# A state-space, attention and feed-forward kernel: recurrence steps spread differently over the stages, its carry copy on another engine, and larger weights for the gap in the feed-forward

## The chip, the cores and the metric

The kernel runs on one core of one Trainium2 chip. The metric is the device time of one execution in microseconds (us); the median of 3 runs before the change is 4947.52 us (4943.62 to 4969.08). The core has five engines [...]: PE (TensorE, matrix products), DVE (VectorE), ACT (ScalarE), POOL (GpSimd) and SP (SyncE, which here issues nearly all transfers). [...]

## The reference, cut to what matters

Input is x, 8 images of 384 channels and 32x32 points, in fp32. Layer 0 normalizes x over channels and runs a selective state-space recurrence (Mamba) over the 1024 points, forwards and backwards, beside a 3x3 depthwise convolution:

```
deltaA  = exp(delta[..., None] * A)                     # 16 states per channel
deltaBu = (delta * u)[..., None] * Bm[:, :, None, :]
h = dA * h + dBu ;  y = einsum('bdn,bn->bd', h, c)      # scan over the points
y = (y + u * D) * silu(z) ;  out = y @ out_proj
x = x + res_scale * ((fwd + bwd) * scale_mod + sigmoid(dwconv(xn)) * xn)
```

Layer 1 takes the points as tokens: t += attention(layernorm(t)) with 6 heads and a causal mask, then t += ffn(layernorm(t)). The feed-forward has weights binarized by sign; after each of its two linear maps the values are scaled by 128 over the largest absolute value of their group and clipped. Groups are 8 // 5 = 1 batch wide, so only batches 0 to 4 pass through it (for 5, 6 and 7 it adds zero). The largest value must be known before the first scaled value can be used: once between the two linear maps, ahead of the gelu, and once after the second.

## The kernel before, in words

Channels lie on the 128 partitions in 3 chunks, points along the free dimension in two halves of 512. Each batch passes four stages:

- *Preparation* (`before_scan`): normalization, input projection (`in`), the short convolution (`u`), gates and the 3x3 convolution (`loc`), the projection to the rows B and C (`xp`), then `delta`, which writes delta and delta times u to DRAM for every chunk, direction and half.
- *Recurrence*: 96 units per batch, 768 in all. A unit is one chunk, one direction, one half and two of the 16 states. POOL multiplies (delta u) by the row of B (`s_first`, L592, out `g`, 128x1024); ACT makes the two exponentials in PSUM (L605, `da`); DVE scans each state (L610, in place in `g`, 128x512); POOL multiplies by the row of C (L616, in place); PE transposes and sums into `y` (`s_sum`, L624). Each direction covers its two halves one after the other (`PARTS`). The units of the first half (24 in a row) begin at zero, and a POOL copy (L615) stores the last column of their two states in `carry`; the units of the second half begin from it. That copy and both products of POOL are pinned: they keep their program order.
- *Attention* (`attention`): output projection (`op`), layernorm, `qp`, `vp`, scores `s`, masked and negated by DVE (L801), exponential by ACT, transposes `pt`, weighting `av`, the factors of the softmax (L831 to L840, small DVE operations), output `ap`.
- *Feed-forward* (`feed_forward`, batches 0 to 4): `hp` (L995), its largest value (`quant_scale`, L961 to L967), gelu by ACT (L1018, four instructions), clip by DVE (L1021), `yp` (L1039), the second scale, and the output.

The recurrence is issued through *slots*. Slot k loads for unit k+4, issues the first product of unit k+2, the exponentials, scans, carry copy and second product of unit k, the sum of unit k-1 and the gate of unit k-2. 98 slots (with 4 that only run ahead) go beside the preparation of the first four batches and the binarizing of the weights, a part that the change leaves as it is. The other 672 are laid over the remaining stages by a plan at the end of the kernel. Every step of a stage is emitted with an estimated duration: 2.5 unless it says otherwise (`emit.of`). The batches go in the order 0, 1, 2, 3, 5, 6, 4, 7. For each the plan appends the steps of attention; for batches 0 to 3 also a *joint* stage, in which the feed-forward steps and the preparation of a later batch (5, 6, 4, 7) are merged by `spread_over`, each list evenly over its own sum of estimates:

```
            fed = spread_over(fed, steps_of(before_scan, later.pop(0), ("pt", "pt", "av")))
            fed = [(f, JOINT * us) for f, us in fed]
```

The estimates of a joint stage are multiplied by JOINT = 0.6. Batch 4 has a feed-forward without a preparation beside it. The attention of batch 7 comes last, with no slots. By the due times (unit 96 i must be done before the attention of the i-th batch) the plan finds the steepest straight line, and along each such line puts slots at even distances in estimated time. A slot thus falls where the sum of the estimates puts it. The tile framework then orders the instructions of each engine, with this order as their priority, except what is pinned or raised by `high_priority`.

Of the kernel before, what the change touches and what calls it, by code (L numbers as in the profile page):

```python
# [38 lines left out]
BC0 = 32  # L39
DW = BC0 + 2 * NS  # L40
PARTS = ((0, 0), (0, 1), (1, 1), (1, 0))
JOINT = 0.6
SET = 8
HURRY = 400
AHEAD = 2
# [9 lines left out]
def kernel(  # L55
# [16 lines left out]
    nc = tc.nc  # L72
    pin = tc.keep_in_program_order
# [25 lines left out]
    def bank(name, tag=None):  # L99
        if tag is None:  # L100
            turn[0] += 1
            tag = ("s", "pt")[turn[0] % 2]
        return ps.tile([P, HB], F32, name=name, tag=tag, bufs=BANKS[tag])
# [7 lines left out]
    def load(dst, src):  # L111
        nc.sync.dma_start(out=dst, in_=src)
# [168 lines left out]
    def layernorm(src, name, emit):  # L281

        dst = src
        st = {}
        for h in range(NH):

            @emit.of(6.0)
            def _(h=h):
                mean = mean_of(lambda c: src()[:, c, half(h)], f"mean_{name}_{h}")
                for c in range(NC):  # L290
                    nc.vector.tensor_tensor(
                        dst()[:, c, half(h)], src()[:, c, half(h)], mean, ALU.subtract
                    )
                st[h] = squares(dst(), h, name)

        for h in range(NH):

            @emit.of(6.0)
            def _(h=h):
                var = mean_of(lambda c: st[h][c], f"var_{name}_{h}")  # L300
                rstd_of(var, 1)
                for c in range(NC):
                    nc.vector.tensor_tensor(  # L303
                        dst()[:, c, half(h)], dst()[:, c, half(h)], var, ALU.mult
                    )
# [289 lines left out]
    def s_scan(u):  # L595
        g = sst["g", u.name]
        key = ("carry", u.b, u.c, u.d)
        begins = u.part % 2 == 0
        if begins and u.n == 0:
            sst[key] = sp.tile([P, NS], F32, name=f"carry_{u.name}", tag="carry", bufs=2 * NC)  # L600
        carry = sst[key]
        for i in range(2):
            n = u.n + i
            da = bank(f"da_{u.name}_{i}", "da")
            nc.scalar.activation(  # L605
                da, sst["dl", u.b, u.c, u.part], AF.Exp, scale=amat[:, u.c, n : n + 1]
            )
            first = 0.0 if begins else carry[:, n : n + 1]
            gi, step = g[:, i, :], -1 if u.d else 1
            nc.vector.tensor_tensor_scan(  # L610
                gi[:, ::step], da[:, ::step], gi[:, ::step], first, ALU.mult, ALU.add
            )
        if begins:
            end = 0 if u.d else HB - 1
            pin(nc.gpsimd.tensor_copy(carry[:, u.n : u.n + 2], g[:, :, end]))  # L615
        pin(nc.gpsimd.tensor_tensor(g, g, sst["bc", 1, u.b, u.part, u.n], ALU.mult))  # L616

    def s_sum(u):
# [351 lines left out]
    def feed_forward(b, t, emit):  # L970
        st = {}

        @emit
        def _():
            st["xn"] = t()
            st["mxh"] = small.tile([P, NF], F32, name=f"mxh_{b}", tag="mxh", bufs=1)
            st["mxy"] = small.tile([P, NC], F32, name=f"mxy_{b}", tag="mxy", bufs=1)

        layernorm(t, f"nf_{b}", emit)
        for m in range(NF):  # L980
            for h in range(NH):

                @emit.of(3.1)
                def _(m=m, h=h):
                    if m % NC == 0 and h == 0:
                        st["h", m // NC] = btile(f"h{m // NC}_{b}")
                    if m % 2 == 0 and h == 0:
                        st["w1"] = mtile(f"w1_{b}_{m}").rearrange("p (c e) -> p c e", c=4)
                        load(
                            st["w1"][:, :NC, :],  # L990
                            w1s[:, m * P : (m + 2) * P].rearrange("(c p) e -> p c e", p=P),
                        )
                    hp = bank(f"hp_{b}_{m}_{h}", "s")
                    for c in range(NC):
                        nc.tensor.matmul(  # L995
                            out=hp,
                            lhsT=st["w1"][:, c, chunk(m % 2)],
                            rhs=st["xn"][:, c, half(h)],
                            start=(c == 0),
                            stop=(c == NC - 1),  # L1000
                        )
                    hm = st["h", m // NC][:, m % NC, :]
                    nc.scalar.activation(hm[:, half(h)], hp, AF.Identity, bias=b1t[:, m : m + 1])
                    if h == NH - 1:
                        nc.vector.tensor_reduce(
                            st["mxh"][:, m : m + 1], hm, AX.X, ALU.max, apply_absolute_value=True
                        )

        @emit.of(3.0)
        def _():  # L1010
            st["s1"] = quant_scale(st["mxh"], f"h_{b}")


        @emit.of(3.0)
        def _():
            with tc.high_priority(offset=60):
                for q in range(NF // NC):
                    pin(nc.scalar.activation(st["h", q], st["h", q], AF.Gelu, scale=st["s1"]))  # L1018
                pin(nc.scalar.preload_act_table_set(LOG_EXP))
                for q in range(NF // NC):  # L1020
                    nc.vector.tensor_scalar(st["h", q], st["h", q], QCLIP, None, ALU.min)  # L1021

        for m in range(NC):
            for h in range(NH):

                @emit.of(10.7)
                def _(m=m, h=h):
                    if m == 0 and h == 0:
                        st["y"] = btile(f"yf_{b}")
                    if h == 0:  # L1030
                        for k in range(0, NF, 6):
                            w = mtile(f"w2_{b}_{m}_{k}", 6 * P).rearrange("p (k e) -> p k e", k=6)
                            load(
                                w, w2s[k * P : (k + 6) * P, chunk(m)].rearrange("(k p) e -> p k e", p=P)
                            )
                            st["w2", k // 6] = w
                    yp = bank(f"yp_{b}_{m}_{h}", "s")
                    for k in range(NF):
                        nc.tensor.matmul(  # L1039
                            out=yp,  # L1040
                            lhsT=st["w2", k // 6][:, k % 6, :],
                            rhs=st["h", k // NC][:, k % NC, half(h)],
                            start=(k == 0),
                            stop=(k == NF - 1),
                        )
                    ym = st["y"][:, m, :]
                    nc.scalar.activation(
                        ym[:, half(h)], yp, AF.Identity, bias=vec[:, m, V_B2 : V_B2 + 1]
                    )
                    if h == NH - 1:  # L1050
                        nc.vector.tensor_reduce(
                            st["mxy"][:, m : m + 1], ym, AX.X, ALU.max, apply_absolute_value=True
                        )

        @emit.of(3.0)
        def _():
            st["s2"] = quant_scale(st["mxy"], f"y_{b}")

        for m in range(NC):

            @emit
            def _(m=m):
                to = mtile(f"t3_{b}_{m}")
                load(to, spilled[b, "t2", m])
                for h in range(NH):
                    ym = bank(f"yq_{b}_{m}_{h}", "s")
                    nc.vector.tensor_scalar(
                        ym, st["y"][:, m, half(h)], st["s2"], QCLIP, ALU.mult, ALU.min
                    )
                    th = to[:, half(h)]  # L1070
                    nc.vector.scalar_tensor_tensor(th, ym, -QCLIP, th, ALU.max, ALU.add)
                nc.sync.dma_start(out=out[b, chunk(m), :], in_=to)


    class Steps(list):
# [4 lines left out]

        def of(self, us):
            return lambda f: self(f, us)

    def spread_over(*lists):

# [64 lines left out]
    for i, b in enumerate(ORDER):  # L1150
        if i > 0:
            due.append((sum(us for _, us in rest), i * per))
        fed = Steps()
        rest += steps_of(attention, b, fed) if i < B - 1 else []
        if fed and later:
            fed = spread_over(fed, steps_of(before_scan, later.pop(0), ("pt", "pt", "av")))
            fed = [(f, JOINT * us) for f, us in fed]
        rest += fed

    timed, here = [], 0  # L1160
# [63 lines left out]
```

## Time and profile before

| | us |
|---|---|
| median of 3 runs | 4947.52 |
| the profiled execution, its own time | 4952.38 |
| its span, first to last instruction | 4950.6 |
| busy PE, DVE, ACT, POOL | 4007.3, 3659.0, 2669.5, 3696.7 |
| start, until the first attention | 829 |
| attention of batches 0, 1, 2, 3, 5, 6 (windows) | 333, 344, 355, 358, 343, 352 |
| joint stages after batches 0, 1, 2, 3 | 324, 327, 315, 328 |
| attention and feed-forward of batch 4 | 322, 210 |
| attention of batch 7, alone | 210 |

An engine's busy time is the time in which one of its instructions runs, its waits for semaphores left out. A group of instructions stands as one line: line of the program, engine, operation, output and inputs by name, shapes, count, then busy time, the mean duration of one, the idle time of the engine just before them and what ended it. The busy shares come in 40 equal slices of the span, as digits in tenths, 9 for 90% and more; a slice is 124 us. The stages in the table were cut at the first output projection of each attention and at the last of its `ap` products.

### The profile page before, as it was taken

How to read it: one execution, taken by the hardware profiler on the slowest of the kernel's cores; microseconds unless marked ns; L12 is line 12 of the kernel's file. 1: busy time of each engine (PE TensorE's matmuls, PEld its weight loads, DVE VectorE, ACT ScalarE, POOL GpSimd, SP SyncE). 2: the span in 40 equal slices, each digit the busy share in tenths (PEclk: the TensorE clock that was granted, in tenths of full speed). 3: DMA queues.
4: the chain of work that ended last, by engine and by line, in shares of the span. 5: the costliest groups of instructions: out<-in, count | busy, mean ns of one | idle time of the engine just before them, and what ended most of it. 6: DMA issues, size and time to landing. Idle time of an engine off the chain costs nothing. (4 is left out here: it accounts for less than half of the span.)

```text
span 4950.6 us, 50616 instructions
## 1 busy us (share of the span) xinstructions
PE 4007.3 (81%) x16362; PEld 2168.0 (44%) x16362; DVE 3659.0 (74%) x4818; ACT 2669.5 (54%) x4855; POOL 3696.7 (75%) x1944
## 2 busy tenths in 40 slices
PE   4677786988788788688887888887887988988889
PEld 1243343544444444344443444443454444444444
DVE  6887878677887778786778967687867677676623
ACT  4565655564654655545655446565456365464425
POOL 0487787996878986768876699867799888888800
PEclk7787796999989899888898998898899989989999
DMA  6554546333454334363343634334643334334210
GB/s 228 204 177 165 196 157 238 107 102 124 150 198 137 115 124 165 126 207 114 108 135 128 220 121 135 111 128 153 203 128 119 114 112 140 117 103 139 92 61 26
DMA packets 365009, 696.35 MB, mean 141 GB/s; under 512 B 30104, under 2 KB 88904, under 8 KB 364744
## 3 DMA queue, kind: packets, MB, share of 16 engines
q1 hardware_dynamic: 355232, 676.97, 41.4%
q10 hardware_dynamic: 9512, 16.15, 0.9%
q8 instruction: 129, 2.11, 0.2%
q14 instruction: 136, 1.11, 0.1%
HBM read 527.33 MB, written 165.68 MB: 140 GB/s over the span
## 5 line engine op out<-in xcount | busy, mean ns | idle before, releaser
L592 POOL TENSOR_TENSOR g<-ud,bc 128x1024 f32<-128x1024 f32 x768 | 1843.2, 2400 | 518.7 <-PE y L624 391.9
L616 POOL TENSOR_TENSOR g<-g,bc 128x1024 f32<-128x1024 f32 x768 | 1821.0, 2371 | 271.1 <-DVE g L610 196.1
L605 ACT ACTIVATE da<-dl,amat 128x512 f32<-128x512 f32 x1536 | 1056.9, 691 | 1457.7 <-DVE g L610 1436.7
L610 DVE TENSOR_TENSOR_SCAN g<-da,g 128x512 f32<-128x512 f32 x768 | 907.5, 1211 | 423.5 <-POOL g L592 411.8
L610 DVE TENSOR_TENSOR_SCAN g<-da,carry,g 128x512 f32<-128x512 f32 x768 | 953.7, 1272 | 348.4 <-POOL g L592 322.9
L624 PE MATMUL y<-ident,g 128*128 128x128 f32 x6144 | 938.7, 301 | 249.2 <-POOL g L616 122.2
L624 PEld LDWEIGHTS y<-ident,g 128*128 128x128 f32 x6144 | 782.0, 155 | 696.7 <-issue 379.8
L787 PE MATMUL s<-k,q 64*128 64x512 f32 (+3 forms) x1152 | 388.4, 600 | 121.6 <-DVE nm L801 103.5
L801 DVE CUSTOM_DVE_ANT_0 pr<-s,cmask 128x512 f32<-128x512 f32 (+3 forms) x576 | 300.3, 546 | 168.4 <-PE s L787 167.1
L811 ACT ACTIVATE pr<-pr,nm 128x512 f32<-128x512 f32 (+3 forms) x576 | 349.9, 609 | 123.6 <-DVE nm L801 121.9
L863 PE MATMUL pt<-ident,pr 128*128 128x128 f32 x1728 | 301.9, 307 | 98.1 <-ACT ptn L866 78.5
L995 PE MATMUL hp<-t,w 128*128 128x512 f32 x720 | 335.7, 611 | 38.7 <-DMA w<-w1s 30.8
L1039 PE MATMUL yp<-h,w 128*128 128x512 f32 x720 | 331.7, 619 | 19.2 <-DMA w<-w2s 15.1
L863 PEld LDWEIGHTS pt<-ident,pr 128*128 128x128 f32 x1728 | 216.2, 154 | 240.2 <-ACT ptn L866 134.5
L877 PE MATMUL av<-ptn,v 128*64 128x512 f32 (+3 forms) x1152 | 270.8, 551 | 49.7 <-ACT ptn L866 35.8
L342 PE MATMUL in<-xn,win 128*128 128x512 f32 x576 | 282.7, 637 | 26.8 <-DVE xc L464 8.2
L866 ACT COPY ptn<-pt 128x512 f32<-128x512 f32 (+3 forms) x576 | 255.6, 474 | 62.0 <-PE pt L863 60.0
L401 DVE SCALAR_TENSOR_TENSOR loc<-xn,vec,loc 128x496 f32<-128x496 f32 (+3 forms) x384 | 259.6, 722 | 20.1 <-ACT loc L390 18.8
L729 PE MATMUL qp<-t,wqk 128*128 128x512 f32 x576 | 263.3, 607 | 10.3 <-DVE t L303 6.5
L615 POOL COPY carry<-g 128x2 f32<-128x2 f32 x384 | 85.7, 223 | 214.8 <-DVE g L610 214.6
L787 PEld LDWEIGHTS s<-k,q 64*128 64x128 f32 x1152 | 132.2, 207 | 257.9 <-DVE nm L801 174.9
L1039 PEld LDWEIGHTS yp<-h,w 128*128 128x128 f32 x720 | 141.8, 201 | 194.0 <-issue 169.8
(151 smaller groups left out, 4714.2 us busy)
## 6 DMA issues: line engine op xcount, KB each, us to landing
bc<-rows SPq DMA_DIRECT2D x512, 512.0 KB, 4.2
dl<-sdl SPq DMA_DIRECT2D x160, 256.0 KB, 3.0
ud<-sud SPq DMA_DIRECT2D x160, 256.0 KB, 2.8
t<-st SPq DMA_DIRECT2D x63, 512.0 KB, 5.0
su<-u SPq DMA_DIRECT2D x48, 512.0 KB, 4.0
du<-su SPq DMA_DIRECT2D x96, 256.0 KB, 3.9
sdl<-du SPq DMA_DIRECT2D x96, 256.0 KB, 2.6
sud<-du SPq DMA_DIRECT2D x96, 256.0 KB, 2.2
```

The costliest lines, as they stand in the source:

```text
L342: nc.tensor.matmul(out=mp, lhsT=st["win", c][:, k, i, :], rhs=st["xn"][:, k, half(h)], start=(k == 0), stop=(k == NC - 1),)
L592: pin(nc.gpsimd.tensor_tensor(g, ud, sst["bc", 0, u.b, u.part, u.n], ALU.mult))
L605: nc.scalar.activation(da, sst["dl", u.b, u.c, u.part], AF.Exp, scale=amat[:, u.c, n : n + 1])
L610: nc.vector.tensor_tensor_scan(gi[:, ::step], da[:, ::step], gi[:, ::step], first, ALU.mult, ALU.add)
L616: pin(nc.gpsimd.tensor_tensor(g, g, sst["bc", 1, u.b, u.part, u.n], ALU.mult))
L624: nc.tensor.matmul(out=y[:, j, :], lhsT=g[:, i, chunk(j)], rhs=ident, is_transpose=True, start=(u.opens and i == 0 and j == 0), stop=(u.cl ...
L787: mm = nc.tensor.matmul(out=ss[e][:, : k1 - k0], lhsT=st["q"][rows_of(e), c, chunk(qi)], rhs=st["k"][rows_of(e), c, k0:k1], start=True, st ...
L801: nc.vector.tensor_tensor_reduce(out=x, in0=ss[e][:, :w], in1=mask, scale=-1.0, scalar=-MASKED, op0=ALU.add, op1=ALU.min, accum_out=m,)
L811: nc.scalar.activation(x, x, AF.Exp, bias=m, scale=-1.0, accum_out=rs[:, i, e, kb : kb + 1])
L863: nc.tensor.transpose(pt[:, chunk(i)], pr[:, e, chunk(j % QT)], ident)
L995: nc.tensor.matmul(out=hp, lhsT=st["w1"][:, c, chunk(m % 2)], rhs=st["xn"][:, c, half(h)], start=(c == 0), stop=(c == NC - 1),)
L1039: nc.tensor.matmul(out=yp, lhsT=st["w2", k // 6][:, k % 6, :], rhs=st["h", k // NC][:, k % NC, half(h)], start=(k == 0), stop=(k == NF - 1),)
```

## The change

Three edits. The carry copy moves from POOL to DVE, and is no longer pinned. JOINT goes from 0.6 to 1.0, so the estimates of a joint stage count in full. And the three steps of the feed-forward that only hold the chain of a scale (the first scale, the gelu with the clip, the second scale) get estimates of a new class Gap: 9, 16 and 9 where each had 3. These weights hold while the feed-forward is merged with a preparation; in the plan of a joint stage they count as SHORT = 3 again. In the feed-forward of batch 4, which is merged with nothing, they count in full.

```diff
-JOINT = 0.6
+JOINT = 1.0
+SHORT = 3.0
...
         if begins:
             end = 0 if u.d else HB - 1
-            pin(nc.gpsimd.tensor_copy(carry[:, u.n : u.n + 2], g[:, :, end]))
+            nc.vector.tensor_copy(carry[:, u.n : u.n + 2], g[:, :, end])
         pin(nc.gpsimd.tensor_tensor(g, g, sst["bc", 1, u.b, u.part, u.n], ALU.mult))
...
-        @emit.of(3.0)
+        @emit.of(Gap(9.0))
         def _():
             st["s1"] = quant_scale(st["mxh"], f"h_{b}")
...
-        @emit.of(3.0)
+        @emit.of(Gap(16.0))
         def _():
             with tc.high_priority(offset=60):
...
-        @emit.of(3.0)
+        @emit.of(Gap(9.0))
         def _():
             st["s2"] = quant_scale(st["mxy"], f"y_{b}")
...
+    class Gap(float):
+        pass
+
...
-            fed = [(f, JOINT * us) for f, us in fed]
+            fed = [(f, JOINT * (SHORT if isinstance(us, Gap) else us)) for f, us in fed]
```

## The prediction

> **What bounds the kernel now.** I read first the busy shares in 40 slices, to see whether one engine carries the whole span:
>
> ```profile
> PE   4677786988788788688887888887887988988889
> DVE  6887878677887778786778967687867677676623
> POOL 0487787996878986768876699867799888888800
> ```
>
> None does. POOL alternates between 9 and 6 or 7 and DVE runs the other way. So I cut the span at the stages (attention from its first output projection to its last `ap` product, feed-forward from there to the next attention) and asked for busy time in these windows. Columns: window, its length, then PE, weight loads, DVE, ACT, POOL busy.
>
> ```profile
> 1486.00:1830.00 344.00, 285.92 (x1376) 162.18 (x1376) 252.18 (x365) 186.63 (x396) 303.21 (x156) 0.91 0.39 128
> 1830.00:2157.00 327.00, 256.17 (x865) 132.95 (x864) 263.28 (x288) 181.91 (x264) 226.74 (x118) 0.88 0.47 152
> ...
> 4208.00:4530.00 322.00, 275.04 (x1311) 154.69 (x1311) 218.80 (x332) 172.52 (x373) 276.55 (x151) 0.92 0.32 104
> 4530.00:4740.00 210.00, 177.31 (x638) 94.76 (x636) 128.37 (x124) 78.89 (x108) 146.54 (x67) 0.95 0.38 120
> ```
>
> An attention stage is nearest to POOL's limit (303 of 344, 0.88; DVE 0.73). A joint stage (feed-forward of one batch beside the preparation of another) is nearest to DVE's (263 of 327, 0.81; POOL 0.69, PE 0.78). The six full attention stages average 347.5 us with 64.7 slots of the recurrence in each (counted by POOL's first products in the windows); the joint ones 323.5 us with 47.
>
> Then the groups of the recurrence, and of the operations that tell what DVE and POOL do to each other (busy us, mean ns, idle before, releaser):
>
> ```profile
> L592 POOL TENSOR_TENSOR g<-ud,bc 128x1024 f32<-128x1024 f32 x768 | 1843.2, 2400 | 518.7 <-PE y L624 391.9 <-DMA ud<-sud 118.7 <-DVE loc L401 5.2
> L610 DVE TENSOR_TENSOR_SCAN g<-da,g 128x512 f32<-128x512 f32 x768 | 907.5, 1211 | 423.5 <-POOL g L592 411.8 <-ACT da L605 10.6
> L615 POOL COPY carry<-g 128x2 f32<-128x2 f32 x384 | 85.7, 223 | 214.8 <-DVE g L610 214.6
> L837 DVE TENSOR_TENSOR rs<-rs,nm 128x16 f32<-128x16 f32 x24 | 40.0, 1668 | 4.5 <-ACT nm L836 4.5
> L840 DVE TENSOR_TENSOR rs<-nm,low 128x16 f32<-128x16 f32 x24 | 31.7, 1322 | 0.7
> ```
>
> L837 and L840 matter most: 16 elements per partition take 1.3 to 1.7 us. By line, their neighbour with one SBUF input takes a tenth:
>
> ```profile
> L837 DVE TENSOR_TENSOR rs<-rs,nm x24: 174/2001/2215, 980.9 to 4918.2; 128x16 f32<-128x16 f32 x24
> L838 DVE TENSOR_REDUCE low<-rs x24: 136/170/171, 982.9 to 4918.4; 128x8 f32<-128x16 f32 x24
> L1021 DVE TENSOR_SCALAR h<-h x20: 1735/2939/12185, 1347.2 to 4660.6; 128x3072 f32<-128x3072 f32 x20
> ```
>
> Laid over POOL's instructions, each long one of these starts while POOL multiplies and ends just after that instruction. L1021 has one input, but shows the same wait.
>
> [...] 174 ns free against a median of 2001. [...] no run shows this copy on DVE yet. [...] Here 2.31 us for a multiply (2.40 recorded) and 0.27 for the carry copy, so 4.62 us per unit and 4.89 with a carry.
>
> **The change part by part.** I need a price for a microsecond on each engine in each stage. My choice: the fourth power of the engine's busy share there (1 where it is the only bound, near 0 where it idles). Check on the trace: one slot is 4.75 us of POOL (half with carry), 2.48 of DVE, 1.2 of PE (76 us of `y` products per 64 slots), 1.38 of ACT. In attention 0.885^4 x 4.75 + 0.72^4 x 2.48 + 0.84^4 x 1.2 + 0.54^4 x 1.38 = 2.9+0.7+0.6+0.1 = 4.3 us a slot. Measured: the attention with 58 slots took 322 us, those with 64.7 took 347.5: 25.5/6.7 = 3.8. I use 3.8 there. In a joint stage: 0.71^4 x 4.75 + 0.82^4 x 2.48 + 0.80^4 x 1.2 + 0.56^4 x 1.38 = 1.2+1.1+0.5+0.1 = 2.9 now; once POOL is at 0.8 and DVE at 0.86 it is 1.9+1.35+0.4+0.1, about 3.75; mean 3.3.
>
> *Slots moved.* The estimates add to 306.5 for an attention, 181.6 for a feed-forward, 180.2 for a preparation. Before, 0.6 x 361.8 = 217.1 stands for a joint stage and the rate is 0.2128 slots per unit: 65.2 and 46.2. After, 361.8 counts in full, the rate is 672/3799.3 = 0.1769: 54.2 and 64.0 (the last feed-forward 35.7 to 36.5). All that a slot issues moves with it: loads on SP's queue, exponentials, scans, products, sums. Six attentions: -10.5 x 3.8 = -40 each, -239; the one with 58: -14; four joint stages: +17 x 3.3 = +56 each, +224. Sum -29. The joint stage's idle POOL covers the multiplies; its DVE (265 busy of 323.5, plus 17 x 2.48 = 42) does not cover the scans fully. SP's extra loads (bc lands in 4.2 us, asked two slots early) lie under a DMA share of 0.5.
>
> *The gap.* Between the last `hp` and first `yp` products PE has some 20 us at 0.35 to 0.6 busy. Heavier weights move about 14 us of preparation into it, and in the last feed-forward about 4 slots. [...] I take -5 for each of five, -25; bounds 0 and -60.
>
> *Carry off POOL.* 384 x 0.27 = 104 us less on POOL, at about 0.45: -47. But the following multiply now waits for DVE's copy[...]: L1021 pushed POOL's next start from 2.31 to 3.71 us. A tiny copy pushes by an estimated 0.1 to 0.2, which gives half back: -24.
>
> *Carry on DVE.* Own cost about 0.15 us (between the 128 ns of the smallest DVE operation here and the 174 ns of L837 free). The wait: at the end of the second scan of a beginning unit, POOL is inside an instruction in 82% of cases and has 0.67 us left on average. That is the lower bound[...]. But the median is 0.19, because scans start at once after the first product, last 2.5 us, and end just before POOL's carry copy plus multiply (2.58) do. Without that POOL copy the multiply ends at 2.31, before the scans, and the DVE copy meets the next one with 2.1 left: upper bound 2.2. Other DVE work loosens the phase; I take 1.0. So 384 x 1.15 = 442 us of DVE. By place: 55 in the start (DVE 425 of 499 once the recurrence runs, 0.85^4 = 0.52): 63 us, +33. 190 in attention at about 0.3: 218 us, +65. 128 in joint stages at 0.86^4 = 0.55: 147 us, +81. 11 in the last feed-forward: +3. Sum +182. [...] 384 x 0.15 x 0.4 = +23. Queued behind a waiting copy are the next unit's scans, attention's masked scores (PE's score products wait for L801 for 103.5 us in all already) and the delta chain. POOL's second product waits for the copy, but starts 6.7 us (median) after the scan today, so that wait is usually covered; where DVE is late it is not, and then y, and the g buffers, are late too.
>
> Sum: -29 - 25 - 24 + 182 = +104. The profiled execution was 4952.4 us (span 4950.6, 1.8 around it), so 5056; the median 4947.5 is 5 lower: 5050.
>
> **The rivals.**
> *A, no lock on the copy* (chance 0.2), the case on the faster side. [...] its wait falls only in time in which DVE had nothing ready. For it: DVE is at 0.72 in attention and waits 735 us for POOL's first product. Against: next after a beginning unit's scans comes another scan in nearly half the cases. -29 - 25 - 47 + 23 = -78: 4870. It decides from the point at which the copies cost less than 78 us, that is below about 0.5 us each.
> *B, DVE becomes the bound of the joint stages* (0.17). There 265 + 42 + 32 x 1.15 = 344 us of DVE, and about 10 more for delta's L530 and L532, which meet a busier POOL. In the start DVE is the bound and reaches 425/499 = 0.85; at that share a joint stage takes 354/0.85 = 416 us, +93. With the masked scores late attention gains only 28 a stage, and the start loses 40: 372 - 168 - 14 + 40 = +230: 5180. Against: both halves of a batch's units alternate, and only one half copies carries.
> *C, nothing moves* (0.13): the scheduler lifts whatever is ready, so the slots land where POOL was free anyway and the waits eat just the gain. 4950 plus or minus 25.
>
> **How the numbers follow.** The forecast (0.5) covers 4980 to 5130, mostly the wait between 0.6 and 1.5 us. The whole range, with A and most of B: 4860 to 5180. Half a percent (25 us) is what this kernel's runs can tell from no change. Faster: A and a part of C, 0.22; same 0.10; slower 0.68.
>
> **What would show it.** Slots: about 54 first products per attention window and 64 per joint one; attention near 310 to 320 us, joint stages near 380 to 395. Lock: L615 as a DVE copy with a mean of about 1.1 us, against 0.2 if A. DVE's share in joint stages up to 0.88 or more. POOL's L616 released by L615, with more idle than the 411 us it and the carry now wait for DVE. The prediction is wrong if copies stay short, or if joint stages take the slots for less than 40 us each.

## The result, and the profile after

The change takes 5021.75 us (median of 4 runs, 5014.89 to 5035.19) against 4945.57 for the kernel before on the same chip: a ratio of 1.0154, interval 1.0122 to 1.0186, some 76 us slower. The profiled execution has a span of 5033.4 us, 82.8 more than before.

First the stage windows of the kernel after, cut as those of before (window, length, busy PE, weight loads, DVE, ACT, POOL): the attention and the joint stage of batch 1, then the attention and the feed-forward of batch 4.

```profile
1528.00:1863.00 335.00, 276.95 (x1313) 152.39 (x1314) 249.95 (x376) 175.89 (x382) 262.60 (x113) 0.91 0.36 119
1863.00:2230.00 367.00, 291.25 (x999) 158.29 (x997) 326.84 (x345) 210.46 (x303) 298.15 (x125) 0.86 0.48 159
...
4296.00:4609.00 313.00, 268.76 (x1289) 149.83 (x1288) 220.91 (x347) 165.90 (x365) 250.93 (x108) 0.93 0.29 95
4609.00:4824.00 215.00, 182.24 (x652) 100.41 (x650) 138.24 (x135) 81.55 (x111) 148.66 (x63) 0.93 0.37 118
```

POOL's busy time in this attention fell from 303 to 263 us, and the stage from 344 to 335. The joint stage went from 327 to 367, its DVE from 263 to 327 busy (0.89 of the window). Over all stages, in us:

| | before | after | difference |
|---|---|---|---|
| start | 830.7 | 841.8 | +11 |
| six attentions (0, 1, 2, 3, 5, 6), mean | 347.4 | 328.9 | 6 x -18.5 = -111 |
| attention of batch 4 | 319.6 | 313.6 | -6 |
| four joint stages, mean | 323.7 | 370.2 | 4 x +46.5 = +186 |
| last feed-forward | 211.4 | 215.0 | +4 |
| last attention | 209.7 | 208.9 | -1 |

That is the whole +83. The first products that POOL starts in the windows are 52 to 56 per attention (63 to 68 before) and 62 to 64 per joint stage (46 to 48).

The groups of the recurrence in the kernel after (lines are one further down than before):

```profile
L593 POOL TENSOR_TENSOR g<-ud,bc 128x1024 f32<-128x1024 f32 x768 | 1842.9, 2400 | 673.2 <-PE y L625 524.3
L617 POOL TENSOR_TENSOR g<-g,bc 128x1024 f32<-128x1024 f32 x768 | 1824.4, 2376 | 495.8 <-DVE carry L616 188.5
L611 DVE TENSOR_TENSOR_SCAN g<-da,g 128x512 f32<-128x512 f32 x768 | 909.1, 1208 | 232.1 <-POOL g L593 213.9
L616 DVE COPY carry<-g 128x2 f32<-128x2 f32 x384 | 361.6, 942 | 5.9
```

The carry copy, two elements per partition, takes DVE 942 ns on average, 361.6 us in all; on POOL it took 223 ns. DVE's scans of beginning units now wait 214 us for POOL's first product where they waited 412, so DVE is less often ahead of POOL. POOL waits longer for PE to release `g` (524 us against 392). The timeline of DVE, then of POOL, shows one copy (start, length, engine, line):

```profile
1970.46 1.19 DVE L611 TENSOR_TENSOR_SCAN g<-da,g 128x512 f32<-128x512 f32 x1
1971.69 2.35 DVE L616 COPY carry<-g 128x2 f32<-128x2 f32 x1
1973.95 1.21 DVE L1006 TENSOR_REDUCE mxh<-h 128x1 f32<-128x1024 f32 x1
```

```profile
1971.66 2.35 POOL L617 TENSOR_TENSOR g<-g,bc 128x1024 f32<-128x1024 f32 x1
1973.96 2.35 POOL L593 TENSOR_TENSOR g<-ud,bc 128x1024 f32<-128x1024 f32 x1
```

POOL's product began 0.03 us before the copy did, and the copy ends with it. The wait lies inside the copy's own duration, so the profile counts it as busy time of DVE. POOL itself goes on at once: it starts its next product 2.30 us later, as ever. Of the 384 copies 244 started while POOL was in an instruction and took 1.39 us on average; 241 of these lasted to the end of that one instruction. The other 140 took 0.16. Where the prediction, the expectations and this text speak of a lock, it stands for this alone: a DVE instruction that lasts until POOL's ends. What holds it there, no trace of this case shows.

### The profile page after: what moved, and what is told of

It reads as the page before. It is cut to its first block, busy times and chain, and to the rows that moved or that the text cites. A ratio compares the mean times of both kernels' runs of the same rounds, so it can differ in the third digit from the quotient of the medians.

```text
span 5033.4 us, 50807 instructions
## 1 busy us (share of the span) xinstructions
PE 4052.4 (81%) x16362; PEld 2181.0 (43%) x16362; DVE 3950.7 (78%) x5192; ACT 2705.4 (54%) x4888; POOL 3623.5 (72%) x1560
## 5 line engine op out<-in xcount | busy, mean ns | idle before, releaser
L593 POOL TENSOR_TENSOR g<-ud,bc 128x1024 f32<-128x1024 f32 x768 | 1842.9, 2400 | 673.2 <-PE y L625 524.3
L617 POOL TENSOR_TENSOR g<-g,bc 128x1024 f32<-128x1024 f32 x768 | 1824.4, 2376 | 495.8 <-DVE carry L616 188.5
L996 PE MATMUL hp<-t,w 128*128 128x512 f32 x720 | 352.7, 636 | 40.2 <-ACT h L1004 23.8
L616 DVE COPY carry<-g 128x2 f32<-128x2 f32 x384 | 361.6, 942 | 5.9
L788 PEld LDWEIGHTS s<-k,q 64*128 64x128 f32 x1152 | 134.8, 202 | 257.4 <-DVE nm L802 192.3
L996 PEld LDWEIGHTS hp<-t,w 128*128 128x128 f32 x720 | 138.7, 203 | 201.2 <-issue 139.9
```

What stands on the lines that cost most here:

```text
L593: pin(nc.gpsimd.tensor_tensor(g, ud, sst["bc", 0, u.b, u.part, u.n], ALU.mult))
L616: nc.vector.tensor_copy(carry[:, u.n : u.n + 2], g[:, :, end])
L788: mm = nc.tensor.matmul(out=ss[e][:, : k1 - k0], lhsT=st["q"][rows_of(e), c, chunk(qi)], rhs=st["k"][rows_of(e), c, k0:k1], start=True, st ...
L996: nc.tensor.matmul(out=hp, lhsT=st["w1"][:, c, chunk(m % 2)], rhs=st["xn"][:, c, half(h)], start=(c == 0), stop=(c == NC - 1),)
```

## The experiments

Each measured number below is a ratio to the kernel before, run on the same chip, with its 95% interval.

**The copy alone, and the plan alone.** The first kernel is the one before with the copy on DVE, the second the change with the copy left on POOL.

```diff
 # e1, from the kernel before
-            pin(nc.gpsimd.tensor_copy(carry[:, u.n : u.n + 2], g[:, :, end]))
+            nc.vector.tensor_copy(carry[:, u.n : u.n + 2], g[:, :, end])
 # e2, from the change
-            nc.vector.tensor_copy(carry[:, u.n : u.n + 2], g[:, :, end])
+            pin(nc.gpsimd.tensor_copy(carry[:, u.n : u.n + 2], g[:, :, end]))
```

> The kernel before with the carry copy on DVE, the plan as before. Theory (the copy waits for POOL's lock, and that is most of the loss): copies of about 0.9 us on average, DVE busy up by 300 us or more, POOL down by 80, and the time up by 60 to 130 us: 5005 to 5075. Rival (the copy is paid by POOL's relief, and the loss is DVE as the bound of the joint stages): 4930 to 4965.

> The change with the carry copy left on POOL, so the plan and the gap alone. Theory: the moved slots about pay for themselves, 4895 to 4960. Rival (joint stages bound by DVE): joint stages at 360 us or more although no copy waits, and 4985 to 5030 in all.

Measured: the copy alone 1.0134 (1.0109 to 1.0159), the plan alone 0.9999 (0.9987 to 1.0010). So nearly all of the loss comes with the copy. The line of the copy in the first of them (min, median, max ns):

```profile
L615 DVE COPY carry<-g x384: 136/812/4515, 141.6 to 4614.7; 128x2 f32<-128x2 f32 x192
```

The rival, DVE as the bound of the joint stages whoever copies, is out as a cause of the net loss: with the plan alone joint stages average 363 us (before 324) and attentions 324 (before 347), which cancel.

**Another form, another engine.** The change again, with two copies of one element each on DVE, and with one copy on ACT.

```diff
-            nc.vector.tensor_copy(carry[:, u.n : u.n + 2], g[:, :, end])
 # e3
+            for i in range(2):
+                nc.vector.tensor_copy(carry[:, u.n + i : u.n + i + 1], g[:, i, end : end + 1])
 # e4
+            nc.scalar.copy(carry[:, u.n : u.n + 2], g[:, :, end])
```

> The change, with the carry copied by DVE as two copies of one element per partition each in place of one of two. [...] each copy takes 0.12 to 0.2 us whatever POOL does, the copies sum to about 120 us, and most of the loss goes: 4900 to 4965. If any DVE copy from SBUF to SBUF waits for POOL, 768 copies wait about 0.6 us each and the time is 5020 or more.

> The change, with the carry copied by ACT[...]. Theory: copies of 0.2 to 0.3 us, 384 of them about 90 us on ACT, no wait on POOL; 4890 to 4960. Rival (joint stages bound by DVE's scans alone): 4985 or more, as with the plan alone.

Measured: 0.9957 (0.9937 to 0.9978) and 0.9949 (0.9933 to 0.9965). The copies by line, of the first and of the second:

```profile
L617 DVE COPY carry<-g x768: 102/145/160, 138.0 to 4530.7; 128x1 f32<-128x1 f32 x192
```

```profile
L616 ACT COPY carry<-g x384: 176/193/209, 139.0 to 4536.5; 128x2 f32<-128x2 f32 x192
```

This decides the form. On the same engine, at the same place in the program, in the same plan, one copy of two elements waits for POOL and two copies of one element never do: no copy of 768 is longer than 160 ns, and 563 of them began while POOL was at work. Why two elements wait and one does not, no run shows. The wait is worth 1.0154 - 0.9957 = 0.0197 of 4948, 97 us (101 against ACT).

Two rivals ride along with such a comparison. The first is that the framework orders the queues anew for every version. The traces speak against it: matched by name, and the carry copies left out, POOL's instructions have the same order in all three versions, DVE's are shifted by 0.4 places on average between the change and the one-element version and by 0.1 between the change and ACT, PE's by 0.1 and 0.3, and ACT's by 2.0 and 1.3. The second is the clock that TensorE was granted, as a share of full speed: a mean of 0.882 in the runs of the change and of 0.888 and 0.890 in these two. A straight line through 35 runs of the kernel before, all on one chip, gives 37 us for 0.01 of clock, so by this estimate 20 to 30 of the 97 to 101 us could go with the clock; whether as a cause or because the engines run differently is not shown.

**The plan in parts.** The weights of the gap with JOINT at 0.6, and JOINT at 1.0 without these weights, both with the copy on POOL.

```diff
 # e5, from the change, with the copy on POOL
-JOINT = 1.0
+JOINT = 0.6
 # e6, from the kernel before
-JOINT = 0.6
+JOINT = 1.0
```

> The kernel before with the weights of the gap alone: JOINT stays at 0.6, the carry copy on POOL. Theory (the gap is worth some us in each of five feed-forwards, as the prediction said): 10 to 40 us faster, 4912 to 4942. Rival (the queues had already lifted ready work into it): within 8 us of the kernel before.

> The kernel before with JOINT at 1.0 alone: no weights of the gap, the carry copy on POOL. The prediction said that the moved slots give 29 us; the plan with the gap gave nothing. If the gap is worth 25 and the slots cost as much, this run is 20 to 40 us slower than before (4972 to 4992); if both are worth nothing it is within 10 us of it.

Measured: 1.0018 (1.0007 to 1.0028) and 1.0062 (1.0045 to 1.0079). The weights alone bring nothing (9 us slower), against what I expected; the moved slots alone cost 31 us, and together they come out even. The weights are thus worth 31 us once the slots have moved, and -9 before that. The windows of batch 1's stages in the second kernel, without waiting copies and without the weights:

```profile
1503.00:1839.00 336.00, 288.28 (x1320) 159.63 (x1321) 233.75 (x353) 177.32 (x382) 266.38 (x137) 0.89 0.36 121
1839.00:2201.00 362.00, 284.41 (x1000) 153.84 (x999) 301.85 (x324) 207.72 (x301) 304.14 (x149) 0.88 0.48 160
```

Its joint stages average 374.1 us with 63.5 slots: +50 for 16.5 slots, 3.1 us a slot. Its attentions average 322.0 with 54.8: -25.4 for 9.9 slots, 2.6 a slot.

**POOL's relief, and a plan between.** The kernel before with the copy on ACT; and the change with the copy on ACT and JOINT at 0.8.

```diff
 # e7, from the kernel before
-            pin(nc.gpsimd.tensor_copy(carry[:, u.n : u.n + 2], g[:, :, end]))
+            nc.scalar.copy(carry[:, u.n : u.n + 2], g[:, :, end])
 # e8, from the change, with the copy on ACT
-JOINT = 1.0
+JOINT = 0.8
```

> The kernel before with the carry copy on ACT and the plan as before. POOL loses 384 x 0.27 = 104 us of work without any lock. The theory that a microsecond of POOL is worth about 0.45 says 47 us faster than before, 4906; if it is worth what the change with ACT gained on the plan alone (26 us), 4925.

> The carry on ACT, the weights of the gap, and JOINT at 0.8, between the two plans (about 59 slots in an attention and 56 in a joint stage). If the price of a slot rises with the load of its stage, the middle is better than both ends: 4895 to 4920. If the price is flat it lies with the change on ACT, 4920 to 4930.

Measured: 0.9916 (0.9899 to 0.9934), 4908.45 us, faster than both kernels of this case; and 0.9939 (0.9916 to 0.9963), which can't be told from JOINT at 1.0. So 104 us less on POOL are worth 42 us in the old plan (0.40 each) and 25 in the new one, 0.9999 - 0.9949. That attention leaves POOL more room in the new plan would explain the difference, but no run isolates it.

**One element on DVE in the old plan.** The kernel before with the two copies of one element.

```diff
-            pin(nc.gpsimd.tensor_copy(carry[:, u.n : u.n + 2], g[:, :, end]))
+            for i in range(2):
+                nc.vector.tensor_copy(carry[:, u.n + i : u.n + i + 1], g[:, i, end : end + 1])
```

> The kernel before with the carry copied by DVE as two copies of one element each, the plan as before. Against the run with one copy of two elements in the same plan (1.0134 of before) it changes the form of the copy alone. Theory: no wait, POOL relieved as with ACT, some 110 us more on DVE: 4910 to 4935. If the place behind the scans on DVE is what hurts, and not the form, it stays above 4980.

Measured: 1.0030 (1.0016 to 1.0043), 4966.28 us, where I expected 4910 to 4935. The form takes three quarters of the loss of the copy alone (1.0134) away, 51 us. But no copy waits here (none is longer than 156 ns), and the version is still some 55 us slower than ACT in this plan, while in the new plan the two were equal. So of the 108 us between a two-element copy on DVE and one on ACT in the old plan, the form explains about half, and the cause of the rest is open. The order of the queues differs little on DVE and PE (shifted by 0.9 and 0.3 places on average against the version with ACT) and more on ACT (4.3).

**Is it DVE's time?** Two kernels keep DVE busy in place of the wait, beside the one-element copies: a reduction of 512 elements whose result nobody uses, first of a tile that is ready early, then of the second scan's own output, so that it must follow the scan and POOL's second product must wait for it.

```diff
 # both, from the change with two copies of one element
+            pad = small.tile([P, 1], F32, name=f"pad_{u.name}", tag="pad")
 # e10
+            nc.vector.tensor_reduce(pad, sst["dl", u.b, u.c, u.part], AX.X, ALU.max)
 # e11
+            nc.vector.tensor_reduce(pad, g[:, 1, :], AX.X, ALU.max)
             for i in range(2):
                 nc.vector.tensor_copy(carry[:, u.n + i : u.n + i + 1], g[:, i, end : end + 1])
```

> The change with two one-element copies and, ahead of them, a reduction of 512 elements from SBUF (about 0.65 us, result unused), so that a beginning unit keeps DVE for about as long as the waiting copy did (0.94 us), without the lock. If the waits cost because they take DVE's time, this is near the change: 5000 to 5030. If what hurts is that the copy's end is tied to the end of POOL's instruction, it is nearer to the version without a wait: 4930 to 4975.

> As the last run, but the reduction (512 elements, about 0.67 us, result unused) reads the second scan's output, so it can't be moved away from behind the scans, and POOL's second product waits for it. If the copies of the change cost because DVE is held behind the scans for about 0.9 us in each beginning unit, the stretches of 24 beginning units take about 148 us as in the change and the run is 5000 to 5030. If it takes the lock (the end of the hold tied to the end of a POOL instruction, and a wait that the order of the queues wasn't made for), they stay near 141 to 144 and the run is 4925 to 4970.

Measured: 0.9962 (0.9947 to 0.9976) and 0.9933 (0.9914 to 0.9952). In the second run the lines of the reduction, of the scans of beginning units and of POOL's first product are

```profile
L617 DVE TENSOR_REDUCE pad<-g x384: 652/681/691, 139.5 to 4524.6; 128x1 f32<-128x512 f32 x192
...
L611 DVE TENSOR_TENSOR_SCAN g<-da,g 128x512 f32<-128x512 f32 x768 | 907.7, 1209 | 231.6 <-POOL g L593 219.4 <-ACT da L606 12.0
L593 POOL TENSOR_TENSOR g<-ud,bc 128x1024 f32<-128x1024 f32 x768 | 1844.4, 2402 | 526.1 <-PE y L628 368.4 <-DMA ud<-sud 120.9 <-DVE o L895 8.2
```

384 x 0.68 = 261 us more of DVE, behind the scans of every beginning unit, and the kernel is no slower than without it. In joint stages DVE is at 0.87 to 0.89, against 0.89 to 0.92 in the change, and the beginning scans wait as little for POOL (219 us, in the change 214). So neither DVE's busy share nor the loss of that slack is by itself what the copies cost. What differs is POOL's wait for PE to release `g`: 368 us here, 442 with one-element copies and 460 with ACT, 524 in the change. The comparison is less clean than the one of the forms, since here the framework did order the queues differently (DVE's shifted by 2.2 places on average against the change, ACT's by 8.8), and the granted clock was higher (0.894 against 0.888 with one-element copies alone), which by the same line is worth an estimated 20 us, far less than 97.

**Half the dose.** Every second copy on ACT, the others on DVE with two elements.

```diff
-            nc.vector.tensor_copy(carry[:, u.n : u.n + 2], g[:, :, end])
+            copy = nc.vector.tensor_copy if u.n % 4 == 0 else nc.scalar.copy
+            copy(carry[:, u.n : u.n + 2], g[:, :, end])
```

> The change with every second carry copy on ACT, the others on DVE with two elements: half the dose of waits. If each wait costs by itself, about half of the difference between the change (1.0154) and the change with ACT (0.9949) remains: 1.003 to 1.008, 4965 to 4990. If DVE falls behind only when the waits come one after another, less: under 4955.

Measured: 1.0061 (1.0041 to 1.0081). The line of the DVE copies:

```profile
L617 DVE COPY carry<-g 128x2 f32<-128x2 f32 x192 | 212.5, 1107 | 2.9
```

From ACT alone (0.9949) to the change (1.0154) that is 0.0112 of 0.0205, 55% of the loss, with half of the copies. They wait longer each than in the change (1107 ns against 942), so they hold 59% of the copies' time (212.5 of 361.6 us). The loss goes about in step with the waiting, as it should if each wait costs by itself and not only a row of them.

**Where the loss sits.** Units come in stretches of 24 that begin at zero and copy, and 24 that take the carry in and don't copy. The time from one second product of POOL to that 24 units later, mean over the stretches behind the first batch (14 that copy, 13 that don't), in us:

| kernel | stretches that copy | that don't |
|---|---|---|
| before | 144.0 | 135.9 |
| copy on ACT, old plan | 141.6 | 134.8 |
| two elements on DVE, old plan | 148.2 | 135.3 |
| one element on DVE, old plan | 144.3 | 135.9 |
| plan alone, copy on POOL | 143.1 | 137.6 |
| change with ACT | 142.2 | 136.2 |
| change with one element on DVE | 141.1 | 136.7 |
| change with the reduction behind the scan | 142.0 | 135.3 |
| change with half the dose | 144.6 | 136.5 |
| the change | 148.1 | 137.5 |

The waiting copies add 5.9 us to a stretch that copies (148.1 against 142.2 on ACT), and 1.3 to one that doesn't. With 16 stretches of each kind that is 94 + 21 = 115 us, near the 101 measured.

What stays open is how a wait that gives DVE's time away harmlessly in the form of a reduction does harm as a wait. Two readings fit. The wait mostly ends with POOL's instruction (241 of 244), so its length follows POOL and not the work that stands behind it on DVE (single copies reach 3.4 us, the reduction 0.69). Or the order of the queues, which is made in advance from estimated durations, allows for a reduction and not for such a wait. No run here separates them.

The wait does not slow POOL directly. Where a copy met POOL at work, POOL's next start follows 2.32 us (median) after the last, against 2.31 wherever POOL goes straight on. In 210 of the 244 cases it came within 2.55 us, and these lost 8 us in all. What POOL's second product waits for the copy itself comes to 188.5 us, against 181.1 with one-element copies and 212.2 with ACT.

## Why the prediction was right

It gave 5050 (4860 to 5180), slower with 0.68; measured 5021.75. The direction and the copy's wait for POOL came as forecast. That the sum came so near is partly luck, because two errors offset. By its steps:

- *The lock*: right in that the copy waits for POOL, and the form of the copy decides (0.9957 against 1.0154). That a copy of this form would wait was the author's estimate: the trace before showed the wait on other operations (L837 at a median of 2001 ns, 174 at the least). L615 was said to take about 1.1 us as a DVE copy; it takes 0.94, and DVE's share in the joint stages rose to between 0.89 and 0.92, as said. One sign failed: POOL's second product was to wait for DVE and the copy for more than 411 us, and it waits 329 (188.5 and 140.5). The loss shows at POOL's first product instead, in the 524 us that it waits for PE (392 before).
- *Carry on DVE, +182*: mis-sized. Measured 97 us against one element and 101 against ACT in the new plan, 51 and 108 in the old one. The wait was 0.94 with its own cost where 1.15 was taken; the phase argument expected the copy to meet a POOL product with 2.1 us left, and only 244 of 384 copies met POOL at work at all. The larger part of the miss is the price: 182/442 = 0.41 us per microsecond of DVE, where 101/362 = 0.28 came out in the new plan. The price by the fourth power of DVE's share failed, since it made any DVE time cost alike; 261 us of plain DVE work at the same place were free.
- *Slots moved, -29*: wrong sign, +31 alone. The joint stage's price was near (3.3 taken, 3.1 measured). The attention's 3.8 a slot came from one attention with 58 slots against six with 64.7, all near POOL's limit; going down to 54.8 it is 2.6, and POOL is then at 0.79 of the window (266 of 336) where it was at 0.88; that this is the reason is argued, not shown. That term was to give 40 us a stage and gave 25.
- *The gap, -25*: right in size only together with the moved slots (-31); alone +9, so the two edits can't be added.
- *Carry off POOL, -24*: with ACT -42 in the old plan, -25 in the new. The half that was to go back, because POOL's next product was to wait for DVE's copy, did not: L1021's push of POOL's next start (2.31 to 3.71 us) is not repeated by a copy of two elements, behind which that start follows at 2.32 us. But with one-element copies in the old plan POOL was relieved as much, and the kernel was 15 us slower than before; why is open.

Slots and gap were forecast 54 us too good (-54 against 0). The copy's two terms were forecast some 80 us too bad: -24 and +182 make +158, and the change stands 77 us above the plan alone. The sum +104 stands against +76 because these errors offset. Of the rivals, A (no lock) would have been 4870; a version without the wait runs 4927. (Its counterargument had a scan next behind a beginning unit's scans in nearly half the cases; the trace before has one in 127 of 384.) B (joint stages of 416 us) did not come: 370. C (nothing moves) did not either: the slots moved as planned and the time left its 25 us, though the plan alone, at 0.9999, looks like C in its sum.

## What to carry to other kernels

Here a DVE copy of two fp32 elements per partition from SBUF to SBUF took 0.16 us while POOL was idle and 1.39 while it worked. Before moving small work from POOL to DVE, look in the trace for tiny DVE operations with microseconds of mean duration (in the kernel before L837, 16 elements per partition, 1668 ns), and where they appear try ACT (192 ns a copy here) or a form with one element (143 ns); ACT was at least as good in both plans (0.9949 against 0.9957, 0.9916 against 1.0030). The busy share of an engine prices a wait badly, since the wait is counted in it (361.6 us of DVE here for 384 copies that take 0.16 us each while POOL is idle); price it from a run that has the same work without the wait. And a price per unit that was read from stages near one bound (3.8 us a slot) need not hold when the load moves away from that bound (2.6).

## What the runs showed of the hardware beyond that

One element per partition instead of two took the same DVE copy from 942 ns (mean) to 143, with POOL's two products equally busy (1842.9 and 1824.4 us in the change, 1844.1 and 1830.2 with one element). In the change a copy that met POOL at work ended with that one POOL instruction in 241 of 244 cases, although in 210 of the 244 POOL started its next one within 2.55 us of the last; POOL's next start hardly moved (2.32 us against 2.31). That is not always so: with half the dose it was 115 of 123, and the longest copy lasted 6.86 us, over three products of POOL. In the kernel before, L1021's longest instruction lasted 12.19 us (its shortest 1.74), while POOL ran five products without a pause, and ended 1.62 us after the fifth.
